# Attention with a feed-forward layer of routed experts on either side: the second layer's shared expert for three more blocks placed behind its experts, the terms of its sums read beside them, and the routing weights carried in the rows

## The chip, the cores and the metric

The kernel runs on one core of a Trainium2 chip. The core has five engines, each with its own instruction stream: TensorE (PE; PEld is its weight load), VectorE (DVE), ScalarE (ACT), GpSimd (POOL) and SyncE (SP), which issues most of the transfers. Sixteen DMA engines move data between the chip's main memory and SBUF, the on-chip memory of 128 partitions; matrix products land in PSUM, eight banks of 128 x 512 floats.

The metric is the device time of one launch in microseconds. Before the change three runs took 3234.64, 3235.33 and 3236.39 us; the median is 3235.33.

## The reference

One row of 4096 tokens of width 256, all in float32. The same feed-forward function (and the same weights) stands before and behind an attention layer:

```
x = x + 0.5 * ffn(layernorm(x))
x = x + attention(layernorm(x))      # 16 heads of 16; qkv with a bias, proj with a bias
x = x + 0.5 * ffn(layernorm(x))

ffn(x): scores = softmax(x @ Wg)                       # 32 experts
        weights, indices = top_k(scores, 4)
        each expert takes its first 2048 (token, k) pairs:
            y[token] += swiglu(x[token], W1[e], W2[e], W3[e]) * weight
        return y + swiglu(x, Ws1, Ws2, Ws3)            # the shared expert, 256 wide
swiglu(x, w1, w2, w3) = silu(x @ w1) * (x @ w3) @ w2
```

## The kernel before

Tokens lie 128 to a tile (`NT` = 32 tiles), and four tiles make a block of 512 (`QB`, `QT`; eight blocks, `NQB`). The kernel goes through these stages; `Layer(0)` is the first feed-forward layer and `Layer(1)` the second.

1. *Front* (`first_front`). x is loaded, normalized and routed (`Layer.route`): VectorE finds the four experts of each token and a slot for each, and POOL scatters each token's row four times into a table of slots in main memory, `xg`, with one indirect DMA for 128 rows (L363). A row (`RW` floats) holds the normalized token, its four experts and, for each, the row of the table `ys` that the result goes to. The weights of the four, halved and set to zero where a pair found no slot, stay in SBUF in `wk` (L347). The shared expert is worked out here too (`shared_half`), added to x, and stored into the fifth row of each token's five in `ys`.
2. *Experts* (`experts`, `run_blocks`). 52 blocks follow each other: 32 of 512 slots, one for each expert, and 20 of 128 for what does not fit. In turn n, `turn` transposes the rows of block n + 1, `first_half` makes the two products and their gate for block n, and `second_half` the third product for block n - 1. Its result leaves PSUM by a VectorE copy (L770) and a ScalarE copy (L768), and POOL scatters it by indirect DMAs into `ys` (L772), 128 rows each. Weights and rows are asked for some turns ahead on SP's queue (L683, L705); SP waits there for the buffers that they go into.
3. *Projections* (`projections`). For each tile the five rows of a token are read back and added, `add_up`: four VectorE operations, each a multiplication by the weight and an addition (L789). Then come normalization, q, k and v.
4. *Attention* (`attention`): eight blocks of queries by four groups of heads by 32 tiles of keys. TensorE makes scores (L1292) and their product with v (L1322), ScalarE the exponentials (L1302). Other work is handed out between these steps in pieces (`front`): after block b is projected (`project_out`, L1401), the routing of b for the second layer goes into the steps of block b + 1. For b of 0 to 2, `Layer.shared` (L375 to L423) follows there: the shared expert, added to x and stored into `ys`. For b of 3 to 5, the block and its transposed rows are only stored, to `x1` and `xTd`.
5. *Tail of attention*. Block 7 is projected and routed, and the shared expert of blocks 3 to 7 is done (`shared_half`, L434 and L456: four first-layer products into four PSUM banks with two tanh; then four VectorE operations; then the second layer in two banks, each followed by an addition).
6. *Second experts*, as 2. They end with a branch (L534) to code that is hardly ever needed.
7. *Last*. For each tile, SP reads the five rows of a token from `ys` (L784, six buffers), VectorE adds them up (L789), and ScalarE's queue stores the result (L1570, L1572).

In most stages the order of work on TensorE, ScalarE, VectorE and SP is the written one (`manual_schedule(engines=ORDERED)`); POOL's is not bound by it. A generator such as `shared_half` is driven by `next`, and each `yield` in it ends a piece, so the calls of `next` are the order on every engine.

Of the kernel before, what the change touches and what calls it, by code (L numbers as in the profile page):

```python
# [18 lines left out]
P = 128  # L19
# [32 lines left out]
LATER = (3, 4, 5, 6)  # L52
PIECES = 28
RW = D + 2 * K
# [6 lines left out]
def kernel(  # L61
# [30 lines left out]
    xTd = dram.tile([len(LATER), P, NC * QB], F32, name="xTd")  # L92
# [93 lines left out]
    class Layer:  # L186


        def __init__(self, index, keep, n, copy):
# [3 lines left out]
            self.wk = keep.tile([P, NT, K], F32, name=f"wk{index}")  # L193
# [10 lines left out]
        def route(self, ch, xt, pool, pm):  # L204
# [48 lines left out]
            for t in range(n):  # L253
# [3 lines left out]
                xr[:, :, D + K :], iota_y[:, :n, :], float(t0 * P * KR), None, ALU.add  # L257
# [89 lines left out]
            nc.vector.tensor_mul(self.wk[:, chunk, :], top[:, :, 0:K], kept[:])  # L347
# [27 lines left out]
        def shared(self, ch, xt, xT, pool, pm):  # L375


            nh = HS // P
            for i0 in range(0, self.n, QT):
                hT = pool.tile([P, nh, QB], F32, tag="shT", name="shT")  # L380
                for hc in range(nh):

                    u = pool.tile([P, QB], F32, tag="u", name="u")
                    for j in range(2):
                        ps = pm.tile([P, QB], F32, tag="m", name="sh_ps")
                        h0 = j * HS + hc * P
                        for c in range(NC):
                            nc.tensor.matmul(  # L388
                                ps[:],
                                ws13_sb[:, c, h0 : h0 + P],  # L390
                                xT[:, c, i0 * P : (i0 + QT) * P],
                                start=(c == 0),
                                stop=(c == NC - 1),
                            )
                        if j == 0:
                            th = pool.tile([P, QB], F32, tag="th", name="th")
                            nc.scalar.activation(th[:], ps[:], AF.Tanh, scale=0.5)
                            nc.vector.scalar_tensor_tensor(
                                u[:], th[:], 1.0, ps[:], ALU.add, ALU.mult
                            )  # L400
                        else:
                            nc.vector.tensor_mul(hT[:, hc, :], u[:], ps[:])
                        yield
                for i in range(0, QT, 2):
                    o = pm.tile([P, 2, D], F32, tag="m", name="so")
                    for j in range(2):
                        for hc in range(nh):
                            nc.tensor.matmul(  # L408
                                o[:, j, :],
                                hT[:, hc, (i + j) * P : (i + j + 1) * P],  # L410
                                ws2_sb[:, hc, :],
                                start=(hc == 0),
                                stop=(hc == nh - 1),
                            )
                    t = i0 + i
                    nc.vector.scalar_tensor_tensor(
                        xt[:, t : t + 2, :], o[:], 0.25, xt[:, t : t + 2, :], ALU.mult, ALU.add
                    )
                    yield
            t0 = ch * self.n  # L420
            nc.sync.dma_start(by_token[:, t0 : t0 + self.n, K, :], xt[:])

        def shared_half(self, xt, xT, t0, pool, pm, bufs=3):  # L423


            nh = HS // P
            made = []
            for hc in range(nh):
# [49 lines left out]
        def clear_low(self, pool):  # L478
# [30 lines left out]
            for i in range(E * n):  # L509
# [4 lines left out]
                    in_offset=None,  # L514
                )

        def experts(self, rare, low):

# [1114 lines left out]
```

## Time and profile before

The profiled execution took 3236.4 us, of which the span (first to last instruction) is 3234.0. Busy times below are microseconds in a stretch; the last column is what the 16 DMA engines moved.

| stretch, us | stage | PE | DVE | ACT | POOL | granted PE clock | GB/s |
|---|---|---|---|---|---|---|---|
| 0 to 217 | front | 138.8 | 140.2 | 37.0 | 127.3 | 0.83 | 188 |
| 217 to 460 | first experts | 228.4 | 105.1 | 67.0 | 161.8 | 0.96 | 244 |
| 460 to 632 | projections | 140.7 | 116.8 | 76.2 | 25.5 | 0.90 | 197 |
| 632 to 2836 | attention | 2200.7 | 378.4 | 2061.0 | 108.2 | 1.00 | 23 |
| 2836 to 2918 | tail of attention | 67.6 | 51.2 | 8.7 | 15.4 | 0.90 | 91 |
| 2918 to 3154 | second experts | 228.7 | 104.2 | 65.8 | 157.1 | 0.98 | 254 |
| 3154 to 3234 | last | 0.0 | 59.4 | 0.0 | 4.8 | 0.53 | 326 |

How to read the profile: a group of instructions is given by its line in the kernel, its engine, its operation and the names of what it writes and reads; "L789 DVE ... 128x256 f32 x192" is 192 executions of line 789 on VectorE. Behind the bar stand the busy time and the mean in ns, and then the idle time just ahead of them and what ended it. The chain of work that ended last is followed back from the last instruction, each time to what released it; an engine's share of this chain says where time can be gained, which its busy time does not. The granted clock is the share of its full clock that TensorE was given.

### The profile page before, as it was taken

The numbers are of one execution on the slowest core, as the hardware profiler recorded it, in microseconds if no ns is written. First come the engines' busy times: TensorE is split into PE (matmuls) and PEld (weight loads), VectorE is DVE, ScalarE is ACT, GpSimd is POOL, SyncE is SP. The second block draws the span as 40 slices with busy tenths as digits, with TensorE's granted clock in tenths as the row PEclk, the third lists the DMA queues.
The fourth block names the chain that finished last, engine by engine and source line by source line (L and its number), as shares of the span: only waits on it lengthen the run. The fifth ranks groups of instructions, "written<-read, shape, count | busy, mean of one in ns | idle before, by whom it ended". The sixth has DMA issues, their size and how long they took to land.

```text
span 3234.0 us, 49972 instructions
## 1 busy us (share of the span) xinstructions
PE 3004.9 (93%) x19947; PEld 1032.3 (32%) x19947; DVE 955.2 (30%) x2820; ACT 2315.7 (72%) x3717; POOL 600.0 (19%) x631
## 2 busy tenths in 40 slices
PE   5769969899999999999999999999999999989990
PEld 3446644322222222222222222222222222246660
DVE  6734458400022112112211210220121131054447
ACT  2112225499989989988998999899999999912220
POOL 3767751000000000100000010010000001015770
PEclk8879989899999999999999999999999999989995
DMA  7367758441100000000000000000000000026768
GB/s 251 132 196 267 264 216 245 118 145 56 39 3 18 15 18 4 28 16 3 18 14 18 18 28 9 17 20 19 3 29 24 3 3 28 1 86 247 270 228 324
DMA packets 139041, 278.22 MB, mean 86 GB/s; under 512 B 32032, under 2 KB 81312, under 8 KB 138400
## 3 DMA queue, kind: packets, MB, share of 16 engines
q1 hardware_dynamic: 101984, 176.15, 16.3%
q0 software_dynamic: 30848, 93.36, 8.0%
q10 hardware_dynamic: 5952, 5.28, 0.5%
q8 instruction: 161, 2.64, 0.3%
q14 instruction: 96, 0.79, 0.1%
HBM read 140.84 MB, written 129.68 MB: 84 GB/s over the span
## 4 chain that ended last, share of the span: by engine, by line
PE 77%; DVE 2%; DMA 1%; issue 1%; SPq 0%; ACT 0%; DVEq 0%
PE banks L1292 34%; PE banks L1322 31%; PE h L742 4%; PE o L764 2%; DVE xt L789 2%; PE xbt_ps L716 1%; PE banks L1401 1%; PE banks L434 1%; PE banks L388 1%; PE banks L456 1%; PE banks L233 0%; PE banks L408 0%; DMA ys<-yb,toi 0%; PE banks L180 0%; PE banks L276 0%
## 5 line engine op out<-in xcount | busy, mean ns | idle before, releaser
L1302 ACT ACTIVATE ex<-banks 128x512 f32<-128x512 f32 (+1 forms) x3224 | 2056.6, 715 | 129.4 <-PE banks L1292 91.9
L1292 PE MATMUL banks<-q,kT 32*128 32x512 f32 x8192 | 1179.3, 642 | 11.9 <-DVE q L1279 11.0
L1322 PE MATMUL banks<-ex,v 128*17 128x512 f32 x8192 | 1079.2, 599 | 0.0
L1292 PEld LDWEIGHTS banks<-q,kT 32*128 32x128 f32 x8192 | 328.4, 184 | 852.8 <-ACT ex L1302 744.6
L363 POOL DMA_INDIRECT xg<-xr,to x128 | 123.6, 965 | 2154.0 <-DVE to L1313 1576.3
L1322 PEld LDWEIGHTS banks<-ex,v 128*17 128x17 f32 x8192 | 136.4, 95 | 777.9 <-issue 776.9
L1343 DVE COPY o<-banks 128x512 f32<-128x512 f32 x32 | 22.1, 692 | 1032.4 <-PE banks L1322 674.1
L772 POOL DMA_INDIRECT ys<-yb,toi x296 | 284.6, 962 | 142.5 <-issue 71.6
L742 PE MATMUL h<-xT,w 128*128 128x512 f32 x512 | 233.3, 599 | 0.0
L768 ACT COPY yb<-o 128x512 f32<-128x512 f32 x64 | 37.5, 586 | 144.2 <-PE o L764 134.8
L363 POOL DMA_INDIRECT xg<-xr,sidx x128 | 124.3, 971 | 78.0 <-DVE st L144 39.3
L751 ACT ACTIVATE s<-h 128x512 f32<-128x512 f32 (+1 forms) x104 | 49.3, 474 | 105.2 <-PE h L742 105.2
L742 PEld LDWEIGHTS h<-xT,w 128*128 128x128 f32 x512 | 93.7, 193 | 93.6 <-issue 93.6
L764 PE MATMUL o<-w,hT 128*128 128x256 f32 x512 | 121.1, 380 | 0.0
L722 ACT COPY xT<-xbt_ps 128x512 f32<-128x512 f32 (+1 forms) x104 | 48.5, 466 | 87.3 <-PE xbt_ps L716 83.4
L1346 DVE RECIPROCAL den<-den 128x512 f32<-128x512 f32 x32 | 107.3, 3353 | 1.1
L753 DVE TENSOR_TENSOR hT<-s,h 128x512 f32<-128x512 f32 (+1 forms) x104 | 55.5, 534 | 158.7 <-PE h L742 155.1
L764 PEld LDWEIGHTS o<-w,hT 128*128 128x128 f32 x512 | 94.4, 191 | 21.3 <-issue 11.5
L1313 DVE SCALAR_TENSOR_TENSOR to<-ex,slot 128x2 int32<-128x2 f32 x56 | 9.0, 161 | 298.7 <-ACT ex L1302 298.7
L789 DVE SCALAR_TENSOR_TENSOR xt<-y,wk,xt 128x256 f32<-128x256 f32 x192 | 95.1, 495 | 6.9
L716 PE MATMUL xbt_ps<-ident,xb 128*128 128x128 f32 x512 | 71.1, 283 | 26.6 <-DMA xb<-xg 25.4
L720 DVE COPY xT<-xbt_ps 128x512 f32<-128x512 f32 (+1 forms) x104 | 55.7, 535 | 89.5 <-PE xbt_ps L716 89.5
(251 smaller groups left out, 1801.9 us busy)
## 6 DMA issues: line engine op xcount, KB each, us to landing
y<-ys SPq DMA_DIRECT2D x64, 640.0 KB
xb<-xg SPq DMA_DIRECT2D x62, 528.0 KB
w<-in_wexp_dram SPq DMA_DIRECT2D x64, 384.0 KB
xg<-zeros SPq DMA_DIRECT2D x148, 132.0 KB
xg<-zero SPq DMA_DIRECT2D x32, 264.0 KB
xbb<-xg SPq DMA_DIRECT2D x40, 132.0 KB
ys<-yb,toi POOLq DMA_INDIRECT x296, 4.2
q<-qd SPq DMA_DIRECT2D x128, 34.0 KB
```

The lines of the kernel that those rows point to most:

```text
L363: ins = nc.gpsimd.indirect_dma_start(out=self.xg[:], out_offset=bass.IndirectOffsetOnAxis(ap=to[:, k : k + 1], axis=0), in_=xr[:, t, :], i ...
L716: nc.tensor.transpose(tp[:, i * P : (i + 1) * P], xb[:, i, c * P : (c + 1) * P], ident[:])
L720: nc.vector.tensor_copy(xT[:, c, : n * P], tp[:, : n * P])
L742: nc.tensor.matmul(ps[:, : n * P], w[:, (j * NC + c) * H : (j * NC + c + 1) * H], xT[:, c, : n * P], start=(c == 0), stop=(c == NC - 1),)
L753: nc.vector.tensor_mul(hT[:, : n * P], s1[:, : n * P], h[1][:, : n * P])
L764: nc.tensor.matmul(o[:, i, :], hT[:, (i0 + i) * P : (i0 + i + 1) * P], w2, start=True, stop=True)
L772: ins = nc.gpsimd.indirect_dma_start(out=ys[:], out_offset=bass.IndirectOffsetOnAxis(ap=b["toi"][:, i : i + 1], axis=0), in_=yb[:, i, :], ...
L789: nc.vector.scalar_tensor_tensor(xt, y[:, k, :], self.wk[:, t, k : k + 1], y[:, K, :] if k == 0 else xt, ALU.mult, ALU.add,)
L1292: nc.tensor.matmul(pm.all[:, banks[j], :], kT[rows, g, t * P : (t + 1) * P], q[rows, :], start=True, stop=True,)
L1302: nc.scalar.activation(ex[:, i : i + n, :], pm.all[:, k : k + n, :], AF.Exp, scale=SCALE)
L1322: nc.tensor.matmul(acc[j * HP : j * HP + HV, :], v[:, t, g * HG + j, :], ex[:, j, :], start=(t == 0), stop=(t == NT - 1),)
L1346: nc.vector.reciprocal(den[:], den[:])
```

## The change

- Rows grow from 264 to 268 floats (`RW`): `route` writes the four weights into the row, and `wk` is gone. `turn` picks, beside the target row, the weight that belongs to its expert. `second_half` multiplies with it where it copied: one VectorE product with a broadcast operand, and two ScalarE operations of 128x256 (one for each tile, since the scale is one number for each partition) in place of one copy of 128x512. What reaches `ys` is weighted already.
- `add_up` is three plain additions for a pair of tiles, and reads come in pairs (`fetch`).
- Blocks 0 to 2 are treated in attention as 3 to 5 were: stored to `x1` and `xTd`, with no shared expert. `Layer.shared` is gone.
- In the second layer the shared expert's sum for blocks 3 to 7 goes to `x1` and no longer to `ys`. While the second experts run, SP loads all of `x1` into `x_all` (eight loads of 512 KB) and the transposed rows of blocks 0 to 2 (three of 512 KB), one at every third turn from the ninth.
- The last stage does the shared expert of blocks 0 to 2 around the sums: pieces ahead of the first sum and four more between sums. It reads four rows of a token in place of five, begins with the tiles of block 3 and ends with those of blocks 0 to 2, and stores two tiles at a time.

```diff
+LATEST = (0, 1, 2)
-RW = D + 2 * K
+RW = D + 3 * K
...
-    xTd = dram.tile([len(LATER), P, NC * QB], F32, name="xTd")
+    xTd = dram.tile([NQB - 2, P, NC * QB], F32, name="xTd")
...
-            self.wk = keep.tile([P, NT, K], F32, name=f"wk{index}")
...
-                xr[:, :, D + K :], iota_y[:, :n, :], float(t0 * P * KR), None, ALU.add
+                xr[:, :, D + K : D + 2 * K], iota_y[:, :n, :], float(t0 * P * KR), None, ALU.add
...
-            nc.vector.tensor_mul(self.wk[:, chunk, :], top[:, :, 0:K], kept[:])
+            nc.vector.tensor_mul(xr[:, :, D + 2 * K :], top[:, :, 0:K], kept[:])
...
-        def shared(self, ch, xt, xT, pool, pm):
...
-            nc.sync.dma_start(by_token[:, t0 : t0 + self.n, K, :], xt[:])
-        def shared_half(self, xt, xT, t0, pool, pm, bufs=3):
+        def shared_half(self, xt, xT, dest, pool, pm, bufs=3):
...
                 nc.vector.scalar_tensor_tensor(part, o[:], 0.25, part, ALU.mult, ALU.add)
-            nc.sync.dma_start(by_token[:, t0 : t0 + QT, K, :], xt)
+            if dest is not None:
+                nc.sync.dma_start(dest, xt)
...
-        def experts(self, rare, low):
+        def experts(self, rare, low, beside=()):
...
-                    self.run_blocks(blocks, pool, ps)
+                    self.run_blocks(blocks, pool, ps, beside)
...
-        def run_blocks(self, blocks, pool, ps):
+        def run_blocks(self, blocks, pool, ps, beside=()):
             made = []
+            beside = dict(zip(range(9, len(blocks), 3), beside, strict=False))
...
+                if n in beside:
+                    beside[n]()
...
-            pair = pool.tile([P, S0 // P, K], F32, tag="pair", name="pair")
-            nc.vector.scalar_tensor_tensor(
-                pair[:, :n], xb[:, :, D : D + K], b["e"], xb[:, :, D + K :], ALU.is_equal, ALU.mult
-            )
-            to = pool.tile([P, S0 // P], F32, tag="to", name="to")
-            nc.vector.tensor_reduce(to[:, :n], pair[:, :n], AX.X, ALU.add)
+            pair = pool.tile([P, 2, S0 // P, K], F32, tag="pair", name="pair")
+            for j in range(2):
+                c0 = D + (j + 1) * K
+                nc.vector.scalar_tensor_tensor(
+                    pair[:, j, :n],
+                    xb[:, :, D : D + K],
+                    b["e"],
+                    xb[:, :, c0 : c0 + K],
+                    ALU.is_equal,
+                    ALU.mult,
+                )
+            to = pool.tile([P, 2, S0 // P], F32, tag="to", name="to", bufs=6)
+            nc.vector.tensor_reduce(to[:, :, :n], pair[:, :, :n], AX.X, ALU.add)
             toi = pool.tile([P, S0 // P], I32, tag="toi", name="toi", bufs=12)
             slot = iota_s[:] if n > 1 else iota_p[:]
             nc.vector.scalar_tensor_tensor(
-                toi[:, :n], slot, float(b["r"]), to[:, :n], ALU.add, ALU.max
+                toi[:, :n], slot, float(b["r"]), to[:, 0, :n], ALU.add, ALU.max
             )
+            b["weight"] = to[:, 1, :]
...
                     )
+                weight = b["weight"][:, i0 : i0 + m]
                 if i0 % 4:
-                    nc.scalar.copy(yb[:, i0 : i0 + m, :], o[:, :m, :])
+                    for i in range(m):
+                        nc.scalar.activation(
+                            yb[:, i0 + i, :], o[:, i, :], AF.Identity, scale=weight[:, i : i + 1]
+                        )
                 else:
-                    nc.vector.tensor_copy(yb[:, i0 : i0 + m, :], o[:, :m, :])
+                    nc.vector.tensor_tensor(
+                        yb[:, i0 : i0 + m, :],
+                        o[:, :m, :],
+                        weight.unsqueeze(2).to_broadcast([P, m, D]),
+                        ALU.mult,
+                    )
...
-        def finished(self, pool, t, xt):
-            y = pool.tile([P, KR, D], F32, tag="y", name="y")
-            nc.sync.dma_start(y[:], by_token[:, t, :, :])
-            self.add_up(y, t, xt)
-        def add_up(self, y, t, xt):
-            for k in range(K):
-                nc.vector.scalar_tensor_tensor(
-                    xt,
-                    y[:, k, :],
-                    self.wk[:, t, k : k + 1],
-                    y[:, K, :] if k == 0 else xt,
-                    ALU.mult,
-                    ALU.add,
-                )
+    def fetch(pool, t, bufs, m=2, rows=KR):
+        y = pool.tile([P, 2, rows, D], F32, tag="y", name="y", bufs=bufs)
+        for i in range(0, 2, m):
+            nc.sync.dma_start(y[:, i : i + m], by_token[:, t + i : t + i + m, :rows, :])
+        return y
+    def add_up(y, xt, to=None):
+        nc.vector.tensor_add(y[:, :, 0:2], y[:, :, 0:2], y[:, :, 2:4])
+        nc.vector.tensor_add(y[:, :, 0], y[:, :, 0], y[:, :, 1])
+        nc.vector.tensor_add(xt, y[:, :, 0], y[:, :, K] if to is None else to)
...
                         xTs[ch][:, :, i * QB : (i + 1) * QB],
-                        h * QT,
+                        by_token[:, h * QT : (h + 1) * QT, K, :],
...
-            def fetch(t):
-                y = pool.tile([P, KR, D], F32, tag="y", name="y", bufs=6)
-                nc.sync.dma_start(y[:], by_token[:, t, :, :])
-                return y
+            ahead = 6
             ys_of = {}
             def begin(c):
                 xt = pool.tile([P, QT, D], F32, tag="x", name="xt")
-                for i in range(QT):
-                    layer.add_up(ys_of.pop(c * QT + i), c * QT + i, xt[:, i, :])
-                    if c * QT + i + 6 < NT:
-                        ys_of[c * QT + i + 6] = fetch(c * QT + i + 6)
+                for i in range(0, QT, 2):
+                    t = c * QT + i
+                    add_up(ys_of.pop(t), xt[:, i : i + 2, :])
+                    if t + ahead < NT:
+                        ys_of[t + ahead] = fetch(pool, t + ahead, ahead // 2)
...
-            for t in range(6):
-                ys_of[t] = fetch(t)
+            for t in range(0, ahead, 2):
+                ys_of[t] = fetch(pool, t, ahead // 2, m=1 if t < QT else 2)
...
-                    if b not in LATER:
-                        yield from layer.shared(b, xt, layer.xT, pool, pm)
-                    elif b < NQB - 2:
+                    if b < NQB - 2:
-                            xTd[b - LATER[0]], layer.xT[:].rearrange("p c q -> p (c q)")
+                            xTd[b], layer.xT[:].rearrange("p c q -> p (c q)")
...
             def half(b, xt, xT):
-                halves[b] = layer.shared_half(xt, xT, b * QT, pool, pm, bufs=2)
+                halves[b] = layer.shared_half(
+                    xt, xT, x1_at[:, b * QT : (b + 1) * QT, :], pool, pm, bufs=2
+                )
                 flat = both[:].rearrange("p j q -> p (j q)")
-                nc.sync.dma_start(flat[:, :n], xTd[b - LATER[0]])
+                nc.sync.dma_start(flat[:, :n], xTd[b])
...
-    layer.experts(layer.more, False)
+    held = ctx.enter_context(tc.tile_pool(name="held", bufs=1))
+    x_all = held.tile([P, NT, D], F32, name="x_all")
+    xT_of = [held.tile([P, NC, QB], F32, name=f"xT{b}") for b in LATEST]
+    def load_x(b):
+        part = slice(b * QT, (b + 1) * QT)
+        nc.sync.dma_start(x_all[:, part, :], x1_at[:, part, :])
+    def load_xT(b):
+        nc.sync.dma_start(xT_of[b][:].rearrange("p c q -> p (c q)"), xTd[b])
+    loads = [lambda b=b: load_xT(b) for b in LATEST]
+    loads += [lambda b=b: load_x(b) for b in range(NQB)]
+    layer.experts(layer.more, False, loads)
     with (
-        tc.tile_pool(name="last", bufs=6, reuse_waits="tile") as pool,
+        tc.tile_pool(name="last", bufs=2, reuse_waits="tile") as pool,
+        tc.tile_pool(name="ps_l", bufs=8, space=PSUM, reuse_waits="tile") as pm,
         tc.manual_schedule(engines=ORDERED),
     ):
-        ready = []
-        for t in range(NT):
-            xt = pool.tile([P, D], F32, tag="x", name="xt")
-            layer.finished(pool, t, xt[:])
-            ready.append(xt)
-            if t >= 4:
-                nc.scalar.dma_start(x_out[:, t - 4, :], ready[t - 4][:])
-        for t in range(NT - 4, NT):
-            nc.scalar.dma_start(x_out[:, t, :], ready[t][:])
+        halves = [
+            layer.shared_half(x_all[:, b * QT : (b + 1) * QT, :], xT_of[b][:], None, pool, pm)
+            for b in LATEST
+        ]
+        ahead = 6
+        order = [*range(len(LATEST) * QT, NT, 2), *range(0, len(LATEST) * QT, 2)]
+        ys_of = {}
+        def get(i):
+            if i < len(order):
+                ys_of[i] = fetch(pool, order[i], ahead, m=1 if i < 2 else 2, rows=K)
+        def store(i):
+            part = slice(order[i], order[i] + 2)
+            nc.scalar.dma_start(x_out[:, part, :], x_all[:, part, :])
+        for i in range(ahead):
+            get(i)
+        next(halves[0])
+        next(halves[1])
+        next(halves[0])
+        next(halves[0])
+        next(halves[2])
+        between = {1: 1, 2: 1, 4: 2, 5: 2}
+        for i, t in enumerate(order):
+            x_t = x_all[:, t : t + 2, :]
+            add_up(ys_of.pop(i), x_t, x_t)
+            get(i + ahead)
+            if i in between:
+                next(halves[between[i]])
+            if i >= 2:
+                store(i - 2)
+        for i in (len(order) - 2, len(order) - 1):
+            store(i)
```

More of the change, by code (lines that the diff above doesn't have):

```diff
@@ L373, in route @@
             yield
-        def shared(self, ch, xt, xT, pool, pm):
[L378 to L393, printed above, removed]
-                            )
-                        if j == 0:
-                            th = pool.tile([P, QB], F32, tag="th", name="th")
-                            nc.scalar.activation(th[:], ps[:], AF.Tanh, scale=0.5)
-                            nc.vector.scalar_tensor_tensor(
-                                u[:], th[:], 1.0, ps[:], ALU.add, ALU.mult
-                            )
[L401 to L415, printed above, removed]
-                    nc.vector.scalar_tensor_tensor(
[L417 to L420, printed above, removed]
-            nc.sync.dma_start(by_token[:, t0 : t0 + self.n, K, :], xt[:])
@@ L722, in turn @@
                     nc.scalar.copy(xT[:, c, : n * P], tp[:, : n * P])
-            pair = pool.tile([P, S0 // P, K], F32, tag="pair", name="pair")
-            nc.vector.scalar_tensor_tensor(
-                pair[:, :n], xb[:, :, D : D + K], b["e"], xb[:, :, D + K :], ALU.is_equal, ALU.mult
-            )
-            to = pool.tile([P, S0 // P], F32, tag="to", name="to")
-            nc.vector.tensor_reduce(to[:, :n], pair[:, :n], AX.X, ALU.add)
+            pair = pool.tile([P, 2, S0 // P, K], F32, tag="pair", name="pair")
[11 more added lines that the diff above has]
+            nc.vector.tensor_reduce(to[:, :, :n], pair[:, :, :n], AX.X, ALU.add)
             toi = pool.tile([P, S0 // P], I32, tag="toi", name="toi", bufs=12)
@@ L779, in second_half @@
                 tc.add_to_no_dep_group(group, ins)
-        def finished(self, pool, t, xt):
-            y = pool.tile([P, KR, D], F32, tag="y", name="y")
-            nc.sync.dma_start(y[:], by_token[:, t, :, :])
-            self.add_up(y, t, xt)
-        def add_up(self, y, t, xt):
-            for k in range(K):
-                nc.vector.scalar_tensor_tensor(
-                    xt,
-                    y[:, k, :],
-                    self.wk[:, t, k : k + 1],
-                    y[:, K, :] if k == 0 else xt,
-                    ALU.mult,
-                    ALU.add,
-                )
+    def fetch(pool, t, bufs, m=2, rows=KR):
[7 more added lines that the diff above has]
+        nc.vector.tensor_add(xt, y[:, :, 0], y[:, :, K] if to is None else to)
     def first_front(layer, keep, weights):
```

## The prediction

> **What bounds the kernel now.** I read the page first (the slices, the chain that ended last), then that chain in order of time, then the timeline of the end.
>
> ```profile
> span 3234.0 us, 49972 instructions
> PE   5769969899999999999999999999999999989990
> DMA  7367758441100000000000000000000000026768
> PE 77%; DVE 2%; DMA 1%; issue 1%; SPq 0%; ACT 0%; DVEq 0%
> ...
> L789 DVE SCALAR_TENSOR_TENSOR xt<-y,wk,xt 128x256 f32<-128x256 f32 x192 | 95.1, 495 | 6.9
> ```
>
> TensorE carries the chain except at the two ends. In order of time, the first projection product (L1401) after each of query blocks 0 to 6 marks one attention block:
>
> ```profile
> 916.82 1.93 PE banks L1401 x8
> ...
> 1199.69 1.93 PE banks L1401 x8
> ...
> 1482.55 1.93 PE banks L1401 x8
> ...
> 1765.42 1.92 PE banks L1401 x8
> ...
> 2036.78 1.93 PE banks L1401 x8
> ...
> 2308.15 1.93 PE banks L1401 x8
> ```
>
> The first three periods are 282.87, 282.86 and 282.87 us, the next two 271.36 and 271.37. The same chain has L388 and L408 (the shared expert) in the long ones alone. The end, from the timeline and, for the branch L534, the answer on that line:
>
> ```profile
> 3153.56 0.42 DVE L770 COPY yb<-o 128x256 f32<-128x256 f32 x1 [0.79 <-PE o L764]
> 3164.16 55.32 SPq L784 DMA_DIRECT2D y<-ys  x32
> 3168.09 0.48 DVE L789 SCALAR_TENSOR_TENSOR xt<-y,wk 128x256 f32<-128x256 f32 x1 [14.10 <-DMA y<-ys]
> 3170.05 0.48 DVE L789 SCALAR_TENSOR_TENSOR xt<-y,wk 128x256 f32<-128x256 f32 x1
> ...
> 3229.36 1.53 DVE L789 SCALAR_TENSOR_TENSOR xt<-y,wk,xt 128x256 f32<-128x256 f32 x3
> ...
> L534 PEldq EVENT_SEMAPHORE  x2: 51/51/51, 204.8 to 3157.1; - x2
> ```
>
> and a stretch of it (columns: PE, PEld, DVE, ACT, POOL busy with counts, granted clock, DMA share, GB/s):
>
> ```profile
> 3166.00:3216.00 50.00, 0.00 (x0) 0.00 (x0) 45.31 (x98) 0.00 (x0) 0.00 (x0) 0.50 1.03 413
> ```
>
> VectorE then needs 1.96 us for each of 32 token tiles and waits for data once. The stretch says that the transfers are as full: 413 GB/s at a share of 1.03. TensorE does nothing there.
>
> **The change part by part.** The profiled execution took 3236.4 us, its span 3234.0; the median shown is 3235.33, so 1.1 comes off at the end.
>
> *Attention.* Three blocks lose the shared expert: 282.87 - 271.36 = 11.51, three times, **-34.5 us**. The blocks without it already route, store x1 and store xTd, which is just what blocks 0 to 2 become, so SP's two added stores a block are in the 271.36. The slices show TensorE without a gap there, so nothing steps in. What these blocks' ScalarE and VectorE did (two tanh, six passes) goes with it and shortens nothing. Blocks 3 to 7 store to x1 instead of ys, as many bytes.
>
> *Front, first experts, projections.* Rows grow from 264 to 268 floats, 1.5%. The scatters run one per 1.27 us on POOL (0.97 and 0.30 of issue), whatever the row; the weights' product (L347, 175 to 205 ns) was already ahead of them. In projections the sum of four rows becomes three additions a pair, but TensorE sets the pace: xn is ready at 495.07, its transposes start at 497.20. The first pair needs tile 1, which landed at 467.45, and ends near 470.1; the second waits for tile 3 at about 470.7 (bytes at 400 GB/s) and ends at 473.4, against 473.3 now. **0**, between -1 and +1. The five-row reads remain.
>
> *Both expert stages.* VectorE: the eviction by a product costs what the copy does (a product out of PSUM, L753, 688 ns for 128x512; the copy L770 692). Each `turn` gains one small pair operation, 165 to 213 ns, and a longer reduction. ScalarE: one 128x512 copy (586) becomes two scaled 128x256 operations. The trace has none with one pointer. Lower end 384, between 277 (128x128) and 597 (128x512); upper end 588, the 128x256 form with scale and bias pointers (L166). I take the middle, 486, so +0.39 us per expert block. All this lies beside TensorE, whose busy time fills the stage from 2933 on, while DVE and ACT are at 48% and 29% in 2960 to 3000. TensorE waited 1.0 us for ACT and 0.3 for DVE in the whole stage. If that cover went, 64 expert blocks would pay up to 0.93 each (rival 3). **0**.
>
> The Trainium skill (ScalarE: Activation LUTs, the paragraph on the ACTIVATE rate beside the table sets) speaks against splitting: 186 ns fixed, 0.833 ns an element, 93 for a pointer. That is 492 for each half; by it the pair costs 0.40 more per block, by the rows 0.39, and the sum is the same as long as TensorE is the bound.
>
> *Loads beside the second experts.* SP gets 11 loads of 512 KB, at every third block from the ninth, each 0.43 us of issue like its other loads. Each goes behind that turn's weights and rows, so the next weights queue behind it; SP spends 149.5 us of this stage waiting for `o` to free a weight buffer, so 4.7 us of issue are there, and rows are asked for two turns before they are transposed. At 415 GB/s one load takes 1.26 us. The stage's DMA share is 0.77, and TensorE waited for rows only at its start (7.5 us). **0**; if every load landed on the path, 11 x 1.26 = +13.9.
>
> *The end.* POOL's scatters and the first read at 3164.1 stay. TensorE passes the branch at 3157.1, then does halves 0 and 1 of the shared expert. A first layer took 6.87 us at full clock (L434 x16), a second 3.45 (L456 x16). So half 0 is through at 3164.0, half 1 at 3170.9, and only then comes half 0's second layer, to 3174.3. VectorE's adds behind it (690 each) end at 3175.2. In VectorE's order all sums queue behind these adds: the first sum starts at **3175.2 instead of 3168.1**, with six pairs of reads already on the way. ScalarE is through the branch at 3155.9 and needs a table load (1.28) before the first tanh near 3160.5: covered. Should half 0's tanh have to wait for the last scatters' memory (3164.1), this start is unchanged.
>
> A sum per pair: 128x1024, then twice 128x512. From 425 ns (128x256) and 692 (128x512) a 128x1024 addition is 1.23; together 2.6, so 16 x 2.6 = 41.6 against 32 x 1.96 = 62.7. Halves 1 and 2 add 4 x 0.65 + 2 x 0.7 = 4.0 each. Without further waits: 3175.2 + 41.6 + 8.0 = 3224.8.
>
> Two waits come in. Eight PSUM banks hold halves 0 and 1; half 2's second half needs banks of half 1 that VectorE frees after its second sum, at 3181.8. TensorE then finishes half 2 at 3185.2 and half 1's second layer at 3188.7; VectorE wanted its adds over at 3187.0 and gets them at 3189.6, +2.6. Half 2's second layer comes near 3197, after TensorE stood 8.7 us, so at half clock: 7 us instead of 3.45, with one sum to cover it, +3.9. End of VectorE 3231.3. The last store carries a pair: 3.1 us after the last addition now, some 3.4 then: 3234.7, **+0.7**.
>
> The clock can add to it. Its rows, in windows of 3.41 us:
>
> ```profile
> 96.41:99.82 3.41, 2.74 (x17) 1.74 (x17) 3.31 (x7) 3.36 (x7) 2.80 (x3) 1.00 0.75 262
> 99.82:103.23 3.41, 3.41 (x13) 3.14 (x14) 0.14 (x1) 2.45 (x5) 2.50 (x4) 0.50 0.34 124
> ...
> 157.85:161.26 3.41, 0.91 (x3) 0.08 (x1) 3.17 (x11) 0.00 (x0) 2.77 (x3) 1.00 0.33 119
> 161.26:164.67 3.41, 0.00 (x0) 0.00 (x0) 3.24 (x12) 0.00 (x0) 2.53 (x3) 0.50 0.30 107
> ```
>
> A window with 0.91 us of work was followed by half clock, and even one with 2.74 was. TensorE now stands 3.6 us at the branch and 4 us before half 2's second part; a dip costs half a window, 1.7 us, at each. I give each 0.7 and take **+3.1** for the end (0.7 + 2 x 0.7 x 1.7). Without any TensorE wait it is -5.8; with three windows at half clock, as after 2922.6 (back at 2932.9), +7.5.
>
> The Trainium skill (TensorE: Matmul & The Clock Gate, part 1) halves the clock after an idle window of 3.4 us, free-running. By it the gap of 3.6 us almost never holds a whole one, and the end would be about +1.5; the rows above show drops without one, so they decide.
>
> Transfers do not bind the end: 16.8 MB read (four rows, not five; 18 issues instead of 32) and 4.2 stored (16 instead of 32, on ACT's queue), at 415 GB/s, end at 3216.6; the cover is 15 us.
>
> Sum: 3236.4 - 34.5 + 3.1 = 3205.0; less 1.1: **3204 us**.
>
> **The rivals.** (1) VectorE's saving arrives: half clock and banks cost little, the end gains up to 5.8. For it: 21.1 us less of sums. Against it: the written order, in which TensorE's three layers stand before the first sum. 3235.3 - 34.5 - 5.8 = 3195. (2) The loads meet rows and weights. For it: share 0.77 already; against it: the rows' lead of two blocks. From 5 us up to +13.9: 3209 to 3218. (3) Slower: the expert stages pass from TensorE to the evictions, with PSUM banks freed late. Price 0.59 (two ACTs at the upper end) + 0.34 (VectorE's small ones), 0.93 x 64 = 59.5 us: 3263. It decides from (34.5 - 3.1 + 6.5)/64 = 0.59 us per block. Against it: ACT at 29% and waits of 1.3 us in all. (4) The change gives nothing: attention's blocks stay long because something else steps in. The blocks at 271.36 exclude nearly all of it.
>
> **How the numbers follow.** Forecast (the end between -2 and +8) 0.60; rival 1 0.20; rival 2 0.14; rival 3 0.04; rival 4 0.02. The measurement tells 0.2% (6.5 us) from nothing. All but 3 and 4 are faster: 0.94, same 0.02, slower 0.04. Range: from rival 1 with projections at -1, 3194, to the forecast's upper end with half of rival 2's span, 3213.
>
> **What would show it.** Block periods of 271.4 from 916 to 1765; no wait of TensorE for rows or ACT in the second experts; VectorE's first sum 7 us later after the last scatter than now; waits of VectorE for `so` of 2 to 4 us, twice or three times; sums of 2.6 us a pair. It is wrong if expert turns lengthen or if the sums wait for reads.

## The result, and the profile after

The changed kernel takes **3198.49 us** (median of four runs, 3198.31 to 3199.03), the kernel before 3235.61 beside it: ratio **0.9887, 95% interval 0.9871 to 0.9902**, 1.1% faster. The prediction said 3204, with 3194 to 3213 as its range. The profiled execution took 3198.56 us.

From the page of the changed kernel: span, slices of TensorE and of the transfers, the chain that ended last, and two groups.

```profile
span 3196.8 us, 49937 instructions
...
PE   5769969899999999999999999999999999989994
...
DMA  7367768442100000000000000000000000027867
...
DVE 1%; PE 1%; issue 0%; ACT 0%
...
L735 ACT ACTIVATE yb<-o,to 128x256 f32<-128x256 f32 x128 | 53.7, 471 | 144.3 <-PE o L729 129.1
...
L386 PE MATMUL sh_ps<-xT,ws_sb 128*128 128x512 f32 x176 | 81.6, 620 | 4.2 <-PEq L487 4.2
```

The chain adds up to 2%, where it gave TensorE 77% before. That is no change in what bounds the kernel. The chain is followed back from the last instruction, and now that TensorE works in the last stage, it goes through L386 to the branch just ahead of it (L487) and stops there: what it shows are the last 75 us. For the rest one reads landmarks. The first projection products (L1365) after query blocks 0 to 3, from the timeline of TensorE:

```profile
917.07 1.13 PE L1365 MATMUL banks<-wproj_sb,both 128*128 128x256 f32 x4
...
1188.42 1.35 PE L1365 MATMUL banks<-wproj_sb,both 128*128 128x256 f32 x5
...
1459.78 1.56 PE L1365 MATMUL banks<-wproj_sb,both 128*128 128x256 f32 x6
...
1731.13 1.13 PE L1365 MATMUL banks<-wproj_sb,both 128*128 128x256 f32 x4
```

The periods are 271.35, 271.36 and 271.35 us, where they were 282.87. The end, from the timeline of all engines:

```profile
3117.44 0.42 DVE L739 TENSOR_TENSOR yb<-o,to 128x256 f32<-128x256 f32 x1 [0.79 <-PE o L729]
...
3121.63 16.73 PE L386 MATMUL sh_ps<-xT,ws_sb 128*128 128x512 f32 x32 [4.23 <-PEq L487]
...
3128.00 50.24 SPq L759 DMA_DIRECT2D y<-ys  x18
...
3138.20 3.62 PE L408 MATMUL so<-ws_sb,shT 128*128 128x256 f32 x16
...
3140.13 0.69 DVE L416 SCALAR_TENSOR_TENSOR x_all<-so,x_all 128x512 f32<-128x512 f32 x1 [7.90 <-PE so L408]
...
3141.66 7.03 PE L386 MATMUL sh_ps<-xT,ws_sb 128*128 128x512 f32 x16
...
3142.47 1.22 DVE L763 TENSOR_TENSOR y<-y 128x1024 f32<-128x1024 f32 x1
...
3160.97 5.80 PE L408 MATMUL so<-ws_sb,shT 128*128 128x256 f32 x16 [7.27 <-DVE shT L402]
...
3192.68 0.69 DVE L765 TENSOR_TENSOR x_all<-y,x_all 128x512 f32<-128x512 f32 x1
```

Reads of y are issued from 3128.0 on, but VectorE's first sum starts at 3142.47: half 0's two additions (L416) stand ahead of it, and they wait for TensorE, which does both first layers before half 0's second layer. From there VectorE works nearly without a gap to the end.

The two profiled executions, cut at the same landmarks (us):

| stretch | before | after | difference |
|---|---|---|---|
| start to first scores | 634.4 | 635.2 | +0.8 |
| first to last scores | 2200.3 | 2165.3 | -35.0 |
| last scores to first transposes of the second experts | 89.4 | 89.7 | +0.3 |
| first transposes to start of the last eviction | 229.4 | 227.3 | -2.2 |
| start of the last eviction to end of span ("the end" below) | 80.5 | 79.4 | -1.1 |
| outside the span | 2.4 | 1.7 | -0.6 |
| sum | 3236.4 | 3198.6 | -37.8 |

(Differences are taken before rounding. Attention scatters a little: in the kernels below that have the same attention, first to last scores took 2162.6 to 2165.9 us, with the same periods.)

So the end has hardly moved, though 12 us of VectorE's work were put into it and 21 us of its sums were taken out. The experiments ask where those went, and whether what was costed at nothing is free.

### The profile page after: what moved, and what is told of

It is laid out like the page before. It is cut to its first block, busy times and chain, and to the rows that moved or that the text cites. A ratio compares the mean times of both kernels' runs of the same rounds, so it can differ in the third digit from the quotient of the medians.

```text
span 3196.8 us, 49937 instructions
## 1 busy us (share of the span) xinstructions
PE 3004.9 (94%) x19947; PEld 1033.2 (32%) x19947; DVE 928.8 (29%) x2764; ACT 2331.2 (73%) x3784; POOL 600.9 (19%) x631
## 3 DMA queue, kind: packets, MB, share of 16 engines
q8 instruction: 161, 2.64, 0.3%
## 5 line engine op out<-in xcount | busy, mean ns | idle before, releaser
L707 PE MATMUL h<-xT,w 128*128 128x512 f32 x512 | 232.6, 597 | 0.0
L735 ACT ACTIVATE yb<-o,to 128x256 f32<-128x256 f32 x128 | 53.7, 471 | 144.3 <-PE o L729 129.1
L729 PEld LDWEIGHTS o<-w,hT 128*128 128x128 f32 x512 | 94.2, 190 | 21.4 <-issue 11.5
L395 ACT ACTIVATE th<-sh_ps 128x512 f32<-128x512 f32 x22 | 13.1, 598 | 103.8 <-PE sh_ps L386 101.0
L386 PE MATMUL sh_ps<-xT,ws_sb 128*128 128x512 f32 x176 | 81.6, 620 | 4.2 <-PEq L487 4.2
```

Of the source, the lines that this page charges most:

```text
L386: nc.tensor.matmul(ps[:], ws13_sb[:, c, h0 : h0 + P], xT[:, c, :], start=(c == 0), stop=(c == NC - 1),)
L707: nc.tensor.matmul(ps[:, : n * P], w[:, (j * NC + c) * H : (j * NC + c + 1) * H], xT[:, c, : n * P], start=(c == 0), stop=(c == NC - 1),)
L729: nc.tensor.matmul(o[:, i, :], hT[:, (i0 + i) * P : (i0 + i + 1) * P], w2, start=True, stop=True)
L735: nc.scalar.activation(yb[:, i0 + i, :], o[:, i, :], AF.Identity, scale=weight[:, i : i + 1])
```

## Experiments

### The rest of the change without the move

The shared expert of blocks 0 to 2 goes back into attention, as the kernel before had it; the end has none.

```diff
                     yield from layer.route(b, xt, pool, pm)
+                    if b in LATEST:
+                        yield from layer.shared(b, xt, layer.xT, pool, pm)
...
-    loads = [lambda b=b: load_xT(b) for b in LATEST]
-    loads += [lambda b=b: load_x(b) for b in range(NQB)]
+    loads = [lambda b=b: load_x(b) for b in range(NQB)]
...
-        next(halves[0])
...
-                next(halves[between[i]])
```

> The changed kernel with the shared expert of blocks 0 to 2 left in attention, where the kernel before had it, so that only the rest of the change is done: weights in the rows, pair sums, x1 read beside the experts, four rows instead of five. Theory (the move brings three blocks of attention 11.5 us each and costs the end; VectorE's order sets the end): attention's periods go back to 282.87 us, +34.5 against the changed kernel. The end loses its shared expert: first sum when the first read lands, about 3.9 us after it is issued; then the transfers decide (21.0 MB at 415 GB/s is 50.6 us from the first read, less the last store, plus a sum of 2.6 and a tail of 3.4), so the end shrinks from 78.9 to about 65 us. Sum 3198.5 + 34.5 - 14 = 3219 us, between 3215 and 3224. Rival (the end is bound by something that neither the sums nor the shared expert change, so it stays near 79 us): 3233 us. Rival (the saving of 21 us in sums arrives in full whatever the transfers do): the end is about 59 us, 3213 us.

Measured: 3221.58 us, ratio 0.9962 (0.9948 to 0.9977). The attention markers are 282.87 apart again, and the end is 68.5 us, where 65 was expected. So weights in the rows and pair sums alone give 12.0 us at the end, not the 21 by which the sums got shorter. What holds it, from VectorE's waits (columns: what waited, for what; us in total, times, longest):

```profile
DVE y L809 <- DMA y<-ys: 22.1, 15, 15.1
```

15.1 of it stand ahead of the first sum (SyncE issues the first read 10.6 us after the last eviction's start); the other 14 waits are 0.5 us each: VectorE now waits for nearly every read. The move then brings the remaining 3221.6 - 3198.5 = 23.1 us: about 34.5 in attention, less 10.9 at the end (68.5 to 79.4).

### The end without its shared expert

```diff
-        next(halves[0])
...
-        between = {1: 1, 2: 1, 4: 2, 5: 2}
...
-            if i in between:
-                next(halves[between[i]])
```

> The changed kernel without the shared expert of blocks 0 to 2 in the last stage (left out of the computation altogether; the loads for it stay). It prices what the moved work costs where it went. Theory: the first sum starts about 10 us earlier, at the first read's landing, and 12 us of VectorE's work are gone, but the transfers (50.6 us) hold the end at about 65 us: 3184.5 us, between 3181 and 3189; attention and experts as in the changed kernel. Rival (transfers or latency set the end already): 3197 to 3199 us. Rival (all of the 10 us and the 12 us come out): 3176 us.

Measured: 3185.91 us (3185.25 to 3189.38); the end is 68.5 us, as in the first run and again 3.5 above what was expected. The timeline of VectorE:

```profile
3130.69 1.23 DVE L763 TENSOR_TENSOR y<-y 128x1024 f32<-128x1024 f32 x1 [15.09 <-DMA y<-ys]
...
3161.72 1.22 DVE L763 TENSOR_TENSOR y<-y 128x1024 f32<-128x1024 f32 x1 [0.47 <-DMA y<-ys]
...
3164.87 1.22 DVE L763 TENSOR_TENSOR y<-y 128x1024 f32<-128x1024 f32 x1 [0.48 <-DMA y<-ys]
```

A pair takes 3.15 us where VectorE needs 2.59. From 3140 to 3175 the transfers of this run move 410 to 414 GB/s at a share of 1.04; by that, 1.31 MB (a pair read and stored) are 3.2 us. With nothing else to do, VectorE follows the transfers. They put a floor some 10.9 us below the changed kernel's end and are not its bound.

### Sums ahead of half 0's second layer

```diff
         next(halves[0])
         next(halves[1])
         next(halves[0])
-        next(halves[0])
-        next(halves[2])
-        between = {1: 1, 2: 1, 4: 2, 5: 2}
+        between = {1: (1, 0), 2: (1, 2), 5: (2,), 6: (2,)}
...
-            if i in between:
-                next(halves[between[i]])
+            for half in between.get(i, ()):
+                next(halves[half])
```

> The changed kernel with another order in the last stage: two pairs are summed before half 0's second layer and its additions, so VectorE's first sum follows half 0's gate (3132.2 in the changed kernel's profile) instead of its additions (3142.5). Nothing is left out. Theory (VectorE's order sets the end): the ten idle microseconds ahead of half 0's second layer are filled, VectorE then works without a gap from about 3132 on, and the end is 8 to 10 us shorter: 3189.5 us, between 3187 and 3192. Rival (the reads bind): at most 3 us shorter, 3195.5 us or more, and VectorE waits for y instead.

Measured: 3190.72 us (3188.13 to 3193.36), ratio 0.9869 (0.9852 to 0.9885). From the timeline of VectorE and its waits in that stage:

```profile
3130.34 1.23 DVE L763 TENSOR_TENSOR y<-y 128x1024 f32<-128x1024 f32 x1 [1.05 <-DMA y<-ys]
```

```profile
DVE x_all L416 <- PE so L408: 2.3, 2, 1.9
DVE y L763 <- DMA y<-ys: 1.1, 1, 1.1
```

In the changed kernel the first of these waits was 10.4 us (7.9 of it ahead of half 0's first addition). The end is 72.2 us, 7.2 shorter, and 7.8 in the medians: the written order, not the transfers, held the changed kernel's end. The gain at the end is less than the 8 to 10 us that were expected: the first sum starts 9.4 us earlier, but half 2's second layer still comes at half clock, and VectorE waits 2.3 us for it.

### ScalarE's evictions twice

```diff
+                    spare = pool.tile([P, 2, D], F32, tag="spare", name="spare", bufs=1)
+                    for i in range(m if self.index else 0):
+                        nc.scalar.activation(
+                            spare[:, i, :], o[:, i, :], AF.Identity, scale=weight[:, i : i + 1]
+                        )
                     for i in range(m):
                         nc.scalar.activation(
```

> The changed kernel with two more scaled evictions of 128x256 on ScalarE, into a spare tile, ahead of the two that count, in each of the 32 expert blocks of the second expert stage: 0.84 us more of ScalarE a block, 27 us in all, and PSUM banks that come free 0.84 us later. Theory (TensorE sets the pace of the expert stages with room on ScalarE): 0 to +2 us, 3198.5 to 3200.5. Rival (the evictions stand next to the path, so that what the change put on ScalarE was already paid in the stage): +14 to +27 us, 3212 to 3226.

Measured: 3199.14 us (3198.51 to 3200.05). Groups of the second expert stage on ScalarE, and TensorE's waits there:

```profile
L740 ACT ACTIVATE yb<-o,to 128x256 f32<-128x256 f32 x64 | 26.9, 479 | 0.0
L736 ACT ACTIVATE spare<-o,to 128x256 f32<-128x256 f32 x64 | 26.9, 471 | 65.8 <-PE o L729 65.8
```

```profile
PE xbt_ps L672 <- DMA xb<-xg: 7.4, 1, 7.4
```

26.9 us more of ScalarE, and the stage takes 227.3 us, as it did without them. TensorE waits for nothing but the first rows. In this stage ScalarE's part of the eviction could cost twice what the change made it cost.

### The loads: taken away, and taken out of their cover

Two kernels and one of the improved ends (below) first ran on a chip where the kernel before took 3398 us, so they ran again on one like the first, with the changed kernel beside them.

```diff
+    nc.gpsimd.memset(x_all[:], 0.0)
...
-    loads += [lambda b=b: load_x(b) for b in range(NQB)]
```

> The changed kernel without the eight loads of x1 beside the second experts; x_all is set to zero instead, on GpSimd, so the output lacks x itself. The three loads of transposed rows stay. Theory (the loads are hidden by TensorE's work): the expert stage stays at 227.7 us from its first transposes to its last eviction, and the time at 3198.5 us, between 3196.5 and 3200.5. Rival (the loads get in the way of weights and rows): 4.2 MB at 415 GB/s is 10.1 us, so 4 to 10 us shorter, 3188.5 to 3194.5.

> The changed kernel without the eight loads of x1 beside the second experts (x_all set to zero on GpSimd; the output lacks x), again. Theory: where TensorE sets the pace of the expert stage (227.7 us) the loads are free, so the stage and the time stay within 1 us of the changed kernel's; where the stage is held by something else (about 268 us, as on the second chip, where it took 267.5 without these loads and 269.3 with them), 1 to 3 us shorter. Rival: 4 to 10 us shorter everywhere.

```diff
-            beside = dict(zip(range(9, len(blocks), 3), beside, strict=False))
+            for load in beside:
+                load()
+            beside = {}
```

> The changed kernel with all eleven loads in one go ahead of the first weights and rows of the second experts, where nothing covers them, in place of one at every third turn from the ninth. Nothing is left out. It prices the loads without their cover: 5.8 MB at 415 GB/s is 13.9 us, of which some may pass while the first rows are waited for anyway (7.3 us). Theory: +7 to +14 us, 3205.5 to 3212.5, all of it ahead of the first transposes. Rival (the loads are free wherever they stand): 3198.5 us, within 1.5.

> The changed kernel with all eleven loads ahead of the first weights and rows, again. On the second chip the stretch from the last scores to the first expert transposes grew from about 89.9 to 108.1 us and the expert stage shrank by about 4. Theory: here that stretch grows from 89.8 by 13 to 19 us, the expert stage stays at 227.7 where TensorE sets its pace, and the time is 13 to 19 us above the changed kernel's, 3211 to 3218 on a chip like the first. Rival (loads free wherever they stand): within 1.5 us of it.

> The changed kernel itself once more, beside the three runs that were made on a chip where the kernel before took 3398 us and not 3235, so that they have it on their own chip. On a chip like the first: 3198.5 us, 0.9887 of the kernel before, expert stage 227.7 us from its first transposes to its last eviction, end 78.9 us. On a chip like the second: 0.988 to 0.990, expert stage 267 to 270, end 78 to 80.

Measured on the chip like the first: the changed kernel 3197.61 us, without the eight loads 3199.19 (3195.45 to 3201.33), with all eleven ahead 3215.64 (3212.21 to 3217.99). The expert stage takes 227.0, 227.3 and 227.1 us. Taking 4.2 MB away saves nothing. The same loads out of cover cost 18 us, all of it ahead of the first transposes; TensorE's wait for rows, 7.3 us in the changed kernel, becomes

```profile
PE xbt_ps L674 <- DMA xb<-xg: 25.0, 1, 25.0
```

and SyncE's queue shows where the time goes:

```profile
2885.30 0.36 SPq L418 DMA_DIRECT2D x<-xq  x1
2888.29 1.28 SPq L1536 DMA_DIRECT2D xT<-xTd  x3
2889.61 9.98 SPq L1533 DMA_DIRECT2D x_all<-x  x8
2899.64 1.89 SPq L641 DMA_DIRECT2D w<-in_wexp_dram  x2
```

The first load is issued 3.0 us after the last store of the shared expert; in the changed kernel the next item there, the weights, went 0.4 us after it. So the weights follow that store 14.3 us later and not 0.4: 2.6 more of waiting, and 11.3 in which the eleven loads are issued. From the weights' issue to the first transposes it then takes 9.9 us instead of 6.2. Together these are the 17.7 us that the wait for rows grew by. Whether the load waits for that store or for the memory that it goes into, the runs don't tell apart.

On the other chip attention took 2165.2 to 2165.7 us, as on the first, but the first scores came 125 to 136 us later and the second expert stage took 265 to 269 us: 269 with eleven loads beside the experts (the kernel with five pairs on TensorE, below), 267 with three, 265 with none. With all eleven ahead the stretch up to the first transposes was 108.1 us instead of 89 to 90. The medians were 3368.20 us without the eight loads and 3385.27 with all of them ahead, in runs that spread by 14 and 17 us.

So the loads are free where TensorE sets the pace. Whether they cost anything where something else does is not shown: in the same three executions the first expert stage, which is the same code in all three kernels, took 271.6, 267.0 and 263.3 us, so differences of 2 to 4 us in the second stage are within what that chip scatters.

### Pairs summed on TensorE

On top of the early sums, some pairs are summed by products with the identity into PSUM. Five pairs at first, then three.

```diff
-            add_up(ys_of.pop(i), x_t, x_t)
+            if i in (7, 9, 11, 13, 15):
+                y = ys_of.pop(i)
+                total = pm.tile([P, 2, D], F32, tag="m", name="total")
+                for j in range(2):
+                    for k in range(K):
+                        nc.tensor.matmul(
+                            total[:, j, :], ident[:], y[:, j, k, :], start=(k == 0), stop=(k == K - 1)
+                        )
+                nc.vector.tensor_add(x_t, x_t, total[:])
+            else:
+                add_up(ys_of.pop(i), x_t, x_t)
```

> The order of the run with two sums ahead of half 0's second layer, and in addition five of the 16 pairs (every second one from the eighth) are summed by TensorE, four products with the identity for each tile into PSUM, with one VectorE addition of 0.69 us behind them instead of three of 2.6. Nothing is left out. VectorE is relieved of 5 x 1.9 = 9.6 us. Theory (behind VectorE the transfers come next: 1.31 MB for each pair at 415 GB/s is 3.16 us, which is the pace that the run without the shared expert shows): the end goes from 71.8 only to 68.5 to 70 us, 3187.5 to 3189.5. Rival (VectorE alone sets the end): 9 us less, 3181.5. Rival (TensorE, at half clock there, releases the reads' buffers late): no gain or a loss, 3190 or more.

> The two sums ahead of half 0's second layer and five pairs summed by TensorE, again. On the second chip the end took 69.3 us. Theory (transfers come next): end 68.5 to 70 us, 9 to 10.5 us less than the changed kernel beside it, 3188 to 3190 us on a chip like the first. Rival (VectorE alone sets the end): 62 to 64 us, 3183.

Measured: 3361.95 us on the other chip (ratio 0.9879, 0.9859 to 0.9900), where the end was 69.8 us; 3189.87 on the chip like the first (ratio 0.9863, 0.9847 to 0.9879), with an end of 72.7, no better than the early sums alone. The theory's 68.5 to 70 held on the one and failed on the other. The last pair, from the timeline:

```profile
3179.35 0.69 DVE L765 TENSOR_TENSOR x_all<-y,x_all 128x512 f32<-128x512 f32 x1
3179.60 6.77 PE L1574 MATMUL total<-y,ident 128*128 128x256 f32 x16 [2.87 <-DMA y<-ys]
3186.41 0.69 DVE L1577 TENSOR_TENSOR x_all<-x_all,total 128x512 f32<-128x512 f32 x1 [6.37 <-PE total L1574]
```

VectorE is through at 3180.0 and then waits 6.4 us: the last read lands at 3179.6, and TensorE, at half clock, needs 6.8 us for what VectorE does in 2.6. (On the other chip it was 5.4.) So the last pair has to stay on VectorE:

```diff
-            if i in (7, 9, 11, 13, 15):
+            if i in (8, 10, 12):
```

> As the run with five pairs on TensorE, but three (the ninth, eleventh and thirteenth pair), so that the last pair is VectorE's again. With five, TensorE started the last pair when its read had landed and needed 6.8 us for it at half clock, with VectorE waiting 6.4 us; VectorE needs 2.6 for a pair. Theory (transfers come next, the last pair on TensorE alone spoilt it): three pairs relieve VectorE of 5.7 us, more than the 3.7 us by which the order with early sums (72.2 us from the last eviction to the end of the span) stands above the run without the shared expert (68.5), so the end is 68.5 to 69.5 us: 3187 us, between 3185.5 and 3189, on a chip where the kernel before takes 3233. Rival (summing on TensorE gives nothing, since the reads' buffers come free later): 72 us or more, 3190.5 us or more.

Measured: **3187.54 us** (3184.49 to 3187.65), ratio **0.9856 (0.9839 to 0.9874)**, and an end of 67.4 us in the profiled execution, the shortest of the four. This is the lowest median of the complete kernels: 10 us below the changed kernel, 46 below the one before. Its interval overlaps those of five pairs and of the early sums alone. From 3130 to 3175 us the transfers are now full (a share of 0.97 to 1.05 in every 5 us), and VectorE waits 1.3 us for reads and 2.0 for half 2's second layer. The end lies 1.1 below the 68.5 us of the first two runs, so that was a near floor and no hard one.

## Why the prediction was right

**Attention** (-34.5): three times 11.5, measured in the periods; -35.0 from first to last scores. Nothing stepped in, as the blocks that had lost this work already showed. In the first run the periods are 282.87 again.

**Front, first experts, projections** (0, -1 to +1): +0.8.

**Expert stages** (0): the ScalarE eviction took 471 ns against 486 in the prediction, VectorE's product what the copy took. Rival 3 is out: the first stage took 232.6 us where it took 231.8, the second got shorter, and there ScalarE's evictions done twice cost nothing. (The waits of 1.0 and 0.3 us for ACT and DVE that the prediction counted stand at TensorE's weight loads; its products waited for rows alone.) The second stage even gained 2.2 us, which was not foreseen. After its first transposes TensorE stood at half clock for 8.8 us before (2924.1 to 2932.9) and for 4.9 after (2890.2 to 2895.1), and before it had a second wait for rows, of 0.67 us, in that time. All the kernels with the new rows that ran on chips like the first took 226.7 to 227.4 us there. Why their second rows come sooner was not tried.

**Loads** (0, at most +13.9): 0 where they stand. Rival 2's condition, loads that meet rows and weights, did not come about where TensorE sets the pace. Its price was not tried in that place; ahead of the first rows the same loads cost 18, more than the 13.9 that their bytes were put at.

**The end** (+3.1) came to -1.1, and this is the step that failed: three of its four terms are off by 2.4 to 3.4 us, with opposite signs. That their sum came within 4.2 us, and with it the time into the range, is in part luck:

- *First sum.* It was to start 7.1 us later than before, 8.8 if the clock dipped once. After the last eviction it started at 25.0 us instead of 14.5, **10.5 later**. The dip was two windows of half clock and not one: first layers of 16.73 us instead of 13.74, so 3.0 and not 1.7. Besides, the first product came 0.6 us behind the end of the branch (`issue` on the chain); the prediction had it start at once.
- *Banks for half 2* (+2.6): **this wait does not exist**. Half 2's first layer ran at 3141.66 in one go of 7.03 us. The prediction took the banks to be given out in turn, so that the second half of it waits for half 1's. No row names the bank, but the four must have been half 0's own, which its gate and its two additions had freed by 3142.5. VectorE's waits at half 1's additions are 0.2 us.
- *Half 2's second layer at half clock* (+3.9): it did come at half clock (5.80 us instead of 3.45), but VectorE waited **1.3**. Its start was earlier by the wait that did not exist, and a sum stood ahead.
- *Sums* of 2.6 a pair and the tail of 3.4: 1.218 + 0.692 + 0.692 = 2.60, and 3.43. Exact:

```profile
L763 DVE TENSOR_TENSOR y<-y 128x1024 f32<-128x1024 f32 x16 | 19.5, 1218 | 0.0
L764 DVE TENSOR_TENSOR y<-y 128x512 f32<-128x512 f32 x16 | 11.1, 692 | 0.5
L765 DVE TENSOR_TENSOR x_all<-y,x_all 128x512 f32<-128x512 f32 x16 | 11.1, 692 | 0.5
```

Together: +0.7 by the prediction's count without dips, +3.4 for the later start, -2.4 and -2.6 for the two waits, makes -0.9; -1.1 was measured. Of the signs that the prediction named, the waits of VectorE for `so` came out otherwise: one of 7.9 us ahead of the first sum, and no other above 1.03. The transfers' cover, put at 15 us, is about 10.9 by the first two runs.

The profiled time was predicted as 3205.0 and was 3198.6. The end makes 4.2 of the 6.4, the expert stage 2.2, attention 0.5, and less time outside the span 0.6, against 1.1 more in the front and ahead of the experts. The outcome lies between the forecast and rival 1 (the end gains up to 5.8). What rival 1 wanted, the written order refused, as the prediction argued: with another order the same work gains 7.8 us more.

## What to carry to other kernels

Work moved off the bounding stage is not free where it lands: it goes behind or ahead of what is there, and one late piece ahead of a queue (here two additions that wait for another engine) delays everything queued behind it, so the first thing to try is the written order at the new place. Measure the floor by leaving the moved work out: it tells how much an order can win before the next limit (here the transfers) takes over. Cover belongs to a place: the same eleven loads cost nothing under a busy TensorE and 18 us ahead of it.

## What the runs showed of the hardware

- **Half clock comes in whole windows, and once it is there, a window that is far from full keeps it.** Windows of 3.41 us around the branch, and some later ones, in the changed kernel (columns: PE, PEld, DVE, ACT, POOL busy with counts, granted clock, DMA share, GB/s):

```profile
3116.96:3120.37 3.41, 0.45 (x2) 0.04 (x1) 0.42 (x1) 0.70 (x2) 2.76 (x3) 1.00 0.35 129
3120.37:3123.78 3.41, 2.15 (x3) 1.15 (x4) 0.00 (x0) 0.00 (x0) 2.54 (x3) 0.50 0.34 126
3123.78:3127.19 3.41, 3.41 (x5) 1.34 (x5) 0.00 (x0) 0.00 (x0) 0.33 (x1) 0.50 0.10 38
3127.19:3130.60 3.41, 3.41 (x9) 1.49 (x9) 1.53 (x3) 1.19 (x2) 0.00 (x0) 1.00 0.41 118
...
3147.65:3151.06 3.41, 2.38 (x8) 1.08 (x7) 3.34 (x6) 0.00 (x0) 0.00 (x0) 1.00 1.01 389
3151.06:3154.47 3.41, 2.64 (x13) 1.98 (x11) 3.15 (x6) 0.00 (x0) 0.00 (x0) 1.00 0.99 306
3154.47:3157.88 3.41, 0.00 (x0) 0.00 (x0) 3.34 (x4) 0.00 (x0) 0.00 (x0) 1.00 0.84 318
3157.88:3161.29 3.41, 0.32 (x1) 0.32 (x2) 3.31 (x6) 0.00 (x0) 0.00 (x0) 0.50 0.88 285
```

  0.45 us of work in a window, then half clock; 2.15 in that one, then half clock again; 3.41, then full. The gap of 4.23 us therefore cost 3.0 us, not 1.7. How little work drops the full clock is not settled: windows of 2.38 and 2.64 us kept it here, where one of 2.74 lost it in the prediction's rows. So a window that is partly idle does not always cost a dip. The Trainium skill (TensorE: Matmul & The Clock Gate, part 1) asks for an idle window before the clock drops and a busy one before it returns. The return agrees, and so does the drop after 3154.47; the drop at the branch came after a window that was not idle (0.45 us).
- The instruction of the branch takes 3.8 to 4.0 us on TensorE's queue in the changed kernel, in both of its executions, and under 0.1 on the other engines.
- On the other chip the same 128 scatters of the front took the same 0.97 us each, but POOL stood 108 us in "issue" between them and the next, against 31. Attention, whose scatters are far apart, took 2165.2 to 2165.7 us there, against 2165.3 in the changed kernel. What makes the issue slower there was not settled.
